# A graph network on one core: an earlier setup for node order and norms, and a last block cut at sixteen tiles

## The chip, the cores and the metric

The kernel runs on one core of a Trainium2 chip. The metric is the device time of one execution in microseconds (us); smaller is better. Three runs of the kernel before gave 6527.34, 6536.39 and 6536.92 us, so the median is 6536.39. The profile is of one further execution, which took 6532.44 us.

A core has five engines that run their own instruction queues side by side: PE (TensorE, matrix products; its weight loads are listed as PEld), DVE (VectorE), ACT (ScalarE), POOL (GpSimd) and SP (SyncE, which here only starts transfers). A transfer (DMA) is started by an engine's queue and then runs on the DMA engines. SBUF is the on-chip memory of 128 partitions; PSUM holds the results of PE.

## The reference: one mean-aggregating layer, then three attention layers over the same graph

There are 6250 nodes with 64 features and 206250 edges sorted by destination. Cut to what matters:

```python
h = relu(layernorm(x))
msg = relu(concat([h[dst], edge_attr_16]) @ W1 + b1)      # layer 0
x = x + relu(segment_mean(msg, dst) + h @ Wres + bres)
h = relu(layernorm(x))
for l in range(3):                                        # 2, 2 and 1 heads
    q, k, v, e = h @ Wq + bq, h @ Wk + bk, h @ Wv + bv, edge_attr_32 @ We
    alpha = sum(q[dst] * (k[src] + e)) / sqrt(C)
    a = segment_softmax(alpha, dst)
    h = segment_sum(a * (v[src] + e), dst) + h @ Ws + bs
    if l < 2: h = prelu(h)
x = x + h
```

## The kernel before

**Order of nodes.** The kernel sorts the nodes by degree into NB = 49 blocks of 128, one node for each partition, so that a block of high degree has many edge tiles and a block of low degree few (`CAP` from 66 to 22). A tile is one edge of each of the 128 nodes of a block.

**Setup** is the first `with tc.manual_schedule(...)` of `gnn_kernel`. There the instructions of POOL, PE, ACT, DVE and SP run on each engine in the order in which the program text issues them. Its steps, with the lines that the prediction uses:

- SP loads `dst` (`prev`), `x` into `xs`, layer 0's weights, and `src` by tiles (`sf`). It then loads `w0blk` (L167), the 24 pieces of the attention weights `wl` (L240, L241), copies `x` into columns 128 to 191 of the DRAM table `tabx` (L242), loads `dst` moved by one (`cur`, L244), `slope` (L245) and 12 pieces of `wblk` (L249).
- PE spreads the first `dst` of each run of 256 edges over all partitions (L185). ACT (L199) and DVE (L194) count from it where seven groups of nodes begin. POOL fetches those stretches of `dst` with seven indirect transfers (L212) into `got`.
- For each of the seven stretches ACT casts it into `looks` (L229) and DVE finds the nodes' first edges in it (L230). ACT sums the squares for the norms of `x`, 49 of them (L225), two behind each stretch and the rest after a last count (L199); then comes the square root (L236).
- DVE turns first edges into degrees and degrees into classes, and counts the classes (L284). PE sums the counts over partitions (`pc`, L286 and L287). DVE scans (L298 to L303) and gets the place of each node in the order (L308 to L321). In between it takes the reciprocal for the norms (L306) and `negr` (L307).
- DVE builds one-hot matrices `to` (L370), `blk` (L372) and `val` (L375, stored over `raw`), in two parts of 24 and 25 columns. PE multiplies them, 49 products that add up in `pperm` (L379). All are 16-bit, and `to` and `val` are read with a step of 49 elements, 98 bytes. DVE reads the sum (`join`, L382) and makes from it, for every block, where each node's edges start (`at_i`, L383) and which node it is (`num_i`, L386).
- The rows of `x` are normalized and projected in 13 groups of four blocks ("quads"): `norm` on ACT (L335) for even quads and on POOL (L332) for odd ones, `turn` (four transposes on PE, L340, and an ACT copy with a relu, L342), `project` (PE L348, ACT copy L350, transfer to `tabx` L351). Rounds 0 to 3 stand in the program ahead of the first part of the 49 products, 4 to 6 ahead of the second, and 7 to 14 behind `join`.
- `sff`, the tiles of `src` as floats (POOL L254), is transposed by PE in 13 pieces (L398), cast by ACT (L401) and written by SP to the flat list `srcs` (L402). This comes last, behind all quads. POOL at last makes `ws` (L406 to L409).

The program tells the end of SP's transfers through eight counters in turn, so a transfer also waits in SP's queue until the one eight places ahead of it has landed: the third `w0blk` transfer waits for `x`.

**Layer 0** (`layer0`) loads edge features, rows of `tabx` and parts of `srcs` by indirect transfers of POOL (all of them at L466, in `pick`): first `load_e(0)`, `load_x(0)`, `load_e(1)` and so on. DVE begins with two memsets (L642), the checks of degrees (L645 and on), 41 small compares (L659) and a comparison of `prev` with `cur` (L666, L667), and then adds up messages.

**Attention** (`attention`) runs three times over the blocks in the order 0, 48, 1, ..., 47. `fetch` gathers one row of keys and values per tile by an indirect transfer of POOL (L466); `scores` takes chunks of up to eight tiles (PE product L809; DVE L817 to L827), `sums` does the softmax and the weighted sum (ACT L849, DVE L841 to L877), and `process` ends a block (L893 to L909). In layers 1 and 2 the block's result is then projected and written to the next layer's table (L914 to L920), and the next layer's gathers wait for that write. In layer 1 a small cast after each chunk (L830) also stores where the sources stand in the new order. The last block, 47, has 24 tiles, the last of them the node itself, which is not gathered. It is done in two parts whose softmaxes are joined:

```python
chunks[end] = [(t, min(CT, cut - t)) for t in range(0, cut, CT)] + [(cut, CAP[end] - cut)]   # cut = 21
parts = [chunks[b][:-1], chunks[b][-1:]] if b == end else [chunks[b]]
```

so the parts are 8 + 8 + 5 tiles and 3 tiles.

Of the kernel before, what the change touches and what calls it, by code (L numbers as in the profile page):

```python
# [22 lines left out]
F32 = mybir.dt.float32  # L23
BF16 = mybir.dt.bfloat16
I32 = mybir.dt.int32
# [54 lines left out]
assert sum(FIN0) == NB  # L80
# [17 lines left out]
def gnn_kernel(ctx: ExitStack, tc: tile.TileContext, x, src_t, dst_t, dst_row, ea16, ea32, eaT16, eaT32, w, out):  # L98
# [17 lines left out]
    with tc.manual_schedule(engines={getattr(mybir.EngineType, e) for e in ("Pool", "PE", "Activation", "DVE", "SP")}), \  # L116
# [6 lines left out]
        val = raw.bitcast(F16)[:, :4 * NB * NB].rearrange("p (v c b) -> p v c b", v=4, b=NB)  # L123
# [16 lines left out]
        sf = p.tile([P, T], I32, name="sf")  # L140
        nc.sync.dma_start(sf, src_t)
# [11 lines left out]
        nc.vector.memset(eps, 1e-5)  # L153
        iota(P, 0, f=col)
# [6 lines left out]
        make_identity(nc, ident)  # L161
# [4 lines left out]
        for j in range(8):  # L166
            nc.sync.dma_start(k.w0blk[j * 16:(j + 1) * 16, j % 4 * D:(j % 4 + 1) * D], w["L0_gnn_W1"][D:, :])  # L167
        nc.gpsimd.memset(ones, 1.0)
# [7 lines left out]
        for t in k.ht:  # L176
            nc.gpsimd.memset(t[D:D + 1, :], 1.0)

# [5 lines left out]
        for c in range(WR):  # L184
            nc.tensor.matmul(pb[:, c, :NW], first[:, c:c + 1].to_broadcast([NW, P]), ident[:NW, :NW],  # L185
                             start=True, stop=True)
        run = p.tile([P, NG0], F32, name="run")
# [30 lines left out]
        negm = p.tile([P, NB], F32, name="negm")  # L218
        var = p.tile([P, NB], F32, name="var")
        nc.vector.tensor_reduce(negm, xs, axis=AX.X, op=OP.add)  # L220
        nc.vector.tensor_scalar(negm, negm, -1.0 / D, None, op0=OP.mult)

        def squares(b):
            sq = p2.tile([P, D], F32, name="sq0")
            nc.scalar.activation(sq, xs[:, b], AF.Square, bias=negm[:, b:b + 1], accum_out=var[:, b:b + 1])  # L225

        place_i = p.tile([P, NG0, 8], U32, name="place_i")
        for g in range(NG0):
            nc.scalar.copy(looks[:, g, :LOOK], got[g])  # L229
            nc.vector.max_index(place_i[:, g], node[:, SG * g:SG * g + 8], looks[:, g])  # L230
            for b in range(2 * g, 2 * g + 2):
                squares(b)
        signs(got[NG0 - 1], NB, less, [P, LOOK], BF16)
        for b in range(2 * NG0, NB):
            squares(b)
        nc.scalar.activation(var, var, AF.Sqrt, bias=eps[:, 0:1], scale=1.0 / D)  # L236

        for l in range(LAYERS):
            for i, s in enumerate("qkvs"):
                nc.sync.dma_start(wl[l][:D, i * D:(i + 1) * D], w[f"L1_gnn_W{s}{l}"])  # L240
                nc.sync.dma_start(wl[l][D:D + 1, i * D:(i + 1) * D], w[f"L1_gnn_b{s}{l}"][None, :])  # L241
# [3 lines left out]
        nc.sync.dma_start(slope, w["L1_gnn_prelu_a"][None, :].to_broadcast([P, 1]))  # L245
        for l in range(LAYERS):
            nc.gpsimd.memset(k.wblk[l], 0.0)
            for j in range(4):
                nc.sync.dma_start(k.wblk[l][j * 32:(j + 1) * 32, j * D:(j + 1) * D], w[f"L1_gnn_We{l}"])  # L249
# [3 lines left out]
        sff = p.tile([P, T], F32, name="sff")  # L253
        nc.gpsimd.tensor_copy(sff, sf)  # L254
        for t, values in ((k.cap, CAP), (least, LEAST)):
            for v, i, j in runs(values):
                nc.gpsimd.memset(t[:, i:j], float(v))
# [26 lines left out]
        nc.vector.tensor_reduce(cnt, oh, axis=AX.X, op=OP.add)  # L284
        pc = pp.tile([P, 2, CLS], F32, name="pc")
# [18 lines left out]

        negr = p.tile([P, NB], F32, name="negr")
        nc.vector.reciprocal(var, var)  # L306
        nc.vector.tensor_mul(negr, negm, var)  # L307
# [15 lines left out]

        hn = p.tile([P, NB, D], F32, name="hn")
        to_tab = tabx.rearrange("(p b) f -> p b f", b=NB)
        quads = [range(b, min(NB, b + 4)) for b in range(0, NB, 4)]
        pts, rxs = {}, {}

        def norm(q):
            for b in quads[q]:  # L330
                if q % 2:
                    nc.gpsimd.tensor_scalar(hn[:, b], xs[:, b], var[:, b:b + 1], negr[:, b:b + 1],  # L332
                                            op0=OP.mult, op1=OP.add)
                else:
                    nc.scalar.activation(hn[:, b], xs[:, b], AF.Identity, bias=negr[:, b:b + 1], scale=var[:, b:b + 1])  # L335

        def turn(q):
            pts[q] = psum.tile([D, 4 * P], F32, name="pr_t")
            for i, b in enumerate(quads[q]):
                nc.tensor.transpose(pts[q][:, i * P:(i + 1) * P], hn[:, b, :], ident)  # L340
            n = len(quads[q]) * P
            nc.scalar.activation(k.ht[q % 2][:D, :n], pts[q][:, :n], AF.Relu)  # L342

        def project(q):
            po = psum.tile([P, 4, 2 * D], F32, name="pr_o")
            n = len(quads[q])
            for i in range(n):
                nc.tensor.matmul(po[:, i, :], k.ht[q % 2][:, i * P:(i + 1) * P], wn, start=True, stop=True)  # L348
            rx = wp.tile([P, 4, 2 * D], F32, name="rx")
# [3 lines left out]
        def rows_of_x(q):  # L353

            if q < len(quads):
                norm(q)
# [1178 lines left out]
```

## Time and profile before

| stage | from, us | to, us | length | DVE busy | POOL busy |
|---|---|---|---|---|---|
| setup (to the first checks of layer 0) | 0 | 121 | 121.0 | 50.7 | 41.5 |
| layer 0 | 121 | 499.5 | 378.5 | 335.6 | 263.8 |
| attention, layer 1 | 499.5 | 2508.9 | 2009.4 | 1034.1 | 1506.1 |
| attention, layer 2 | 2508.9 | 4518.0 | 2009.1 | 1008.8 | 1505.9 |
| attention, layer 3 | 4518.0 | 6530.7 | 2012.7 | 1339.9 | 1511.1 |

The profiled execution has a span of 6530.7 us and took 6532.44 us, so 1.7 us lie around the span. In a line of the timeline or of a group, "out<-in" names what is written from what, "x12" is a count of instructions, and the bracket at the end tells how long the engine stood idle before it and what ended that wait. "SPq" and "POOLq" are the queues that start transfers. An idle time that is put down to "issue" ended with nothing that the profile shows.

### The profile page before, as it was taken

How to read it: one execution, taken by the hardware profiler on the slowest of the kernel's cores; microseconds unless marked ns; L12 is line 12 of the kernel's file. 1: busy time of each engine (PE TensorE's matmuls, PEld its weight loads, DVE VectorE, ACT ScalarE, POOL GpSimd, SP SyncE). 2: the span in 40 equal slices, each digit the busy share in tenths (PEclk: the TensorE clock that was granted, in tenths of full speed). 3: DMA queues.
4: the chain of work that ended last, by engine and by line, in shares of the span. 5: the costliest groups of instructions: out<-in, count | busy, mean ns of one | idle time of the engine just before them, and what ended most of it. 6: DMA issues, size and time to landing. Idle time of an engine off the chain costs nothing. (4 is left out here: it accounts for less than half of the span.)

```text
span 6530.7 us, 28765 instructions
## 1 busy us (share of the span) xinstructions
PE 1956.0 (30%) x5430; PEld 1204.2 (18%) x5430; DVE 3769.0 (58%) x6686; ACT 366.2 (6%) x1266; POOL 4828.3 (74%) x5159
## 2 busy tenths in 40 slices
PE   5762222222222221221222221222333333333342
PEld 3441111111111111111111111111111211121121
DVE  5984545455555553644455545454766666676775
ACT  3220000000000000000000000000000000000000
POOL 4677777777777776777777777776777777777776
PEclk9775555555555555555555555555666666666665
DMA  3674333333333332222222222222222222222222
GB/s 108 221 234 110 81 88 79 85 85 85 83 81 84 83 81 65 72 70 66 69 68 66 69 69 67 70 69 60 71 65 69 65 67 67 67 66 69 65 67 66
DMA packets 242745, 534.93 MB, mean 82 GB/s; under 512 B 101234, under 2 KB 123218, under 8 KB 241458
## 3 DMA queue, kind: packets, MB, share of 16 engines
q0 software_dynamic: 169792, 372.65, 22.7%
q1 hardware_dynamic: 72764, 160.36, 7.8%
q14 instruction: 143, 1.17, 0.1%
q8 instruction: 46, 0.75, 0.0%
HBM read 460.23 MB, written 74.03 MB: 82 GB/s over the span
## 5 line engine op out<-in xcount | busy, mean ns | idle before, releaser
L466 POOL DMA_INDIRECT kv<-tab,src x4788 | 4518.1, 944 | 1499.9 <-issue 1405.9
L820 DVE TENSOR_TENSOR kv<-kv,pe 128x1024 f32<-128x1024 f32 (+7 forms) x666 | 740.1, 1111 | 2237.1 <-DMA kv<-tab,src 2009.4
L809 PE MATMUL pe<-wblk,ea 128*128 128x256 f32 x1740 | 690.6, 553 | 668.4 <-DVE kv L820 598.5
L940 PE MATMUL pos<-only,is_q 128*128 128x448 f32 x616 | 422.6, 799 | 1092.8 <-DVE only L937 1066.8
L914 PE MATMUL pt<-ident,hn 128*64 128x128 f32 x98 | 41.2, 420 | 2131.7 <-DVE hn L909 2110.8
L809 PEld LDWEIGHTS pe<-wblk,ea 128*128 128x128 f32 x1740 | 492.8, 290 | 926.5 <-DVE kv L820 565.3
L866 DVE TENSOR_REDUCE some<-kv 128x64 f32<-128x512 f32 (+3 forms) x693 | 645.4, 931 | 23.9
L809 PE MATMUL pe<-wblk,eaT 128*128 128x256 f32 x870 | 344.7, 561 | 370.7 <-DVE kv L820 347.0
L827 DVE TENSOR_REDUCE al<-prod 128x16 f32<-128x512 f32 (+7 forms) x693 | 438.7, 633 | 24.1
L826 DVE TENSOR_TENSOR prod<-kv,more 128x512 f32<-128x512 f32 (+3 forms) x693 | 438.4, 633 | 24.0
L862 DVE TENSOR_TENSOR kv<-kv,more 128x512 f32<-128x512 f32 (+3 forms) x693 | 431.0, 622 | 0.0
L914 PEld LDWEIGHTS pt<-ident,hn 128*64 128x64 f32 x98 | 12.6, 128 | 2195.4 <-DVE hn L909 2173.8
L940 PEld LDWEIGHTS pos<-only,is_q 128*128 128x128 f32 x616 | 131.6, 252 | 1281.0 <-issue 1087.7
L809 PEld LDWEIGHTS pe<-wblk,eaT 128*128 128x128 f32 x870 | 246.8, 293 | 452.3 <-DVE kv L820 364.7
L947 DVE TENSOR_TENSOR all<-all,pos 128x448 f32<-128x448 f32 x301 | 186.0, 618 | 143.8 <-PE pos L940 135.7
L849 ACT ACTIVATE more<-al,m 128x37 f32<-128x37 f32 (+18 forms) x250 | 73.0, 292 | 2916.1 <-DVE m L844 2891.7
L543 PE MATMUL pm<-w0blk,eT 64*128 64x256 f32 x868 | 171.0, 514 | 91.8 <-DVE msg L546 77.5
L937 DVE TENSOR_TENSOR only<-is_r,more 128x448 f32<-128x448 f32 x308 | 185.1, 613 | 1.5
L466 POOL DMA_INDIRECT e<-in_ea_dram,at_i x98 | 104.9, 1070 | 102.6 <-PE ps L398 39.9
L568 DVE TENSOR_TENSOR msg<-msg 128x128 f32<-128x128 f32 (+12 forms) x221 | 136.2, 616 | 7.1
L543 PEld LDWEIGHTS pm<-w0blk,eT 64*128 64x128 f32 x868 | 110.1, 249 | 136.4 <-DVE msg L546 72.7
L918 PE MATMUL po<-ws,ht 65*128 65x256 f32 x196 | 118.4, 706 | 34.3 <-ACT ht L916 34.3
(217 smaller groups left out, 1737.9 us busy)
## 6 DMA issues: line engine op xcount, KB each, us to landing
kv<-tab,src POOLq DMA_INDIRECT x4788
ea<-eat SPq DMA_DIRECT2D x26, 576.0 KB, 3.8
ea<-eat SPq DMA_DIRECT2D x24, 512.0 KB, 3.4
ea<-eat SPq DMA_DIRECT2D x16, 640.0 KB, 4.0
ean<-e SPq DMA_DIRECT2D x13, 576.0 KB, 3.7
ea<-ean SPq DMA_DIRECT2D x13, 576.0 KB, 4.4
eat<-eaT SPq DMA_DIRECT2D x13, 576.0 KB, 5.6
ea<-eat SPq DMA_DIRECT2D x16, 448.0 KB, 3.4
```

What stands on the lines that cost most here:

```text
L466: return nc.gpsimd.indirect_dma_start(out=out, out_offset=None, in_=table, in_offset=bass.IndirectOffsetOnAxis(ap=idx, axis=0))
L543: nc.tensor.matmul(pm[:, r, u].rearrange("p j f -> p (j f)"), eT[h, t0 // 8 + u, :], k.w0blk[h, :], start=True, stop=True)
L568: nc.vector.tensor_add(msg[:, :h] if c > 2 else total, msg[:, :h], msg[:, c - h:c])
L809: nc.tensor.matmul(pe[:, 4 * (g - g0):4 * (g - g0) + 4].rearrange("p j f -> p (j f)"), ea[:, g, :], k.wblk[l], start=True, stop=True)
L820: nc.vector.tensor_add(pair(kv[:, :m, :2 * D]), pair(kv[:, :m, :2 * D]), pe[:, :m, None, :].to_broadcast([P, m, 2, D]))
L826: nc.vector.tensor_mul(prod[:, :n], kv[:, :n, :D], q[:, None, :].to_broadcast([P, n, D]))
L827: nc.vector.tensor_reduce(als[b][:, :H, t0:t0 + n].rearrange("p h j -> p j h"), prod[:, :n].rearrange("p j (h c) -> p j h c", h=H), axis=A ...
L862: nc.vector.tensor_mul(v.rearrange("p j (h c) -> p j h c", h=H), v.rearrange("p j (h c) -> p j h c", h=H), ex[:, :H, t0:t0 + n].rearrange( ...
L866: nc.vector.tensor_reduce(some[:, i, :], v.rearrange("p j f -> p f j"), axis=AX.X, op=OP.add)
L937: nc.vector.tensor_mul(only, is_r[:, rs, None].to_broadcast([P, SG, D]), res[:, None, :].to_broadcast([P, SG, D]))
L940: nc.tensor.matmul(pos[i].rearrange("p r f -> p (r f)"), is_q, only.rearrange("p r f -> p (r f)"), start=True, stop=True)
L947: nc.vector.tensor_add(all_[:, rs], all_[:, rs], pos.pop(i - 1))
```

## The change

In setup, `make_identity` moves ahead of the first iota on POOL. The loads of `wl`, `slope` and `wblk` (with POOL's memsets of `wblk`) move up in the program to right behind `w0blk`. POOL casts `sff` ahead of the seven indirect transfers; PE transposes it at once into the four PSUM buffers that the quads use later; and ACT casts the four results one by one behind the stretches 0, 1, 3 and 4, each with its transfer by SP, from two buffers `si` in turn. The mean `negm` moves ahead of the counts. For blocks 17 to 48 DVE sums the squares in three large instructions; ACT does blocks 0 to 16 before the first stretch. The square root stands behind stretch 2, the reciprocal and `negr` behind stretch 4. The quads go in a new order `seq`; rounds 0 to 4 stand ahead of the class sums `pc`, and all others ahead of the one-hot matrices, none between or behind the 49 products. `to` and `val` are stored in groups of eight columns, so that PE reads them with a step of 8 elements, 16 bytes; column 48 has tiles of its own, `to1` and `val1`. The memsets of `cap` and `least` move behind the quads in POOL's order, ahead of `ws`.

In attention, the last block's parts are 8 + 8 tiles and 5 + 3 tiles, and its casts for the sources (layer 1) move behind the block's result.

```diff
@@ setup @@
+        make_identity(nc, ident)
         iota(P, 0, f=col)
...
         for j in range(8):
             nc.sync.dma_start(k.w0blk[j * 16:(j + 1) * 16, j % 4 * D:(j % 4 + 1) * D], w["L0_gnn_W1"][D:, :])
+        for l in range(LAYERS):
+            for i, s in enumerate("qkvs"):
+                nc.sync.dma_start(wl[l][:D, i * D:(i + 1) * D], w[f"L1_gnn_W{s}{l}"])
+                nc.sync.dma_start(wl[l][D:D + 1, i * D:(i + 1) * D], w[f"L1_gnn_b{s}{l}"][None, :])
+        nc.sync.dma_start(slope, w["L1_gnn_prelu_a"][None, :].to_broadcast([P, 1]))
+        for l in range(LAYERS):
+            nc.gpsimd.memset(k.wblk[l], 0.0)
+            for j in range(4):
+                nc.sync.dma_start(k.wblk[l][j * 32:(j + 1) * 32, j * D:(j + 1) * D], w[f"L1_gnn_We{l}"])
...
+        nc.gpsimd.tensor_copy(sff, sf)
...
+        nc.vector.tensor_reduce(negm, xs, axis=AX.X, op=OP.add)
+        nc.vector.tensor_scalar(negm, negm, -1.0 / D, None, op0=OP.mult)
...
+        turned = []
+        for t0 in range(0, T, 4 * P):
+            ps = psum.tile([P, 4, P], F32, name="ps", tag=("pr_t", "pr_o")[t0 // (4 * P) % 2])
+            for i, n in enumerate(whole_tiles):
+                nc.tensor.transpose(ps[:n, i, :], sff[:, t0 + i * P:t0 + i * P + n], ident)
+            turned.append((t0, len(whole_tiles), whole_tiles[-1], ps))
+        def flat_src():
+            t0, n, m, ps = turned.pop(0)
+            si = p2.tile([P, 4, P], I32, name="si")
+            nc.scalar.copy(si[:m, :n], ps[:m, :n])
+            nc.sync.dma_start(srcs[...], si[:m, :n])
+        NS = 17
+        nc.vector.tensor_add(hn[:, NS:], xs[:, NS:], negm[:, NS:, None].to_broadcast([P, NB - NS, D]))
+        nc.vector.tensor_mul(hn[:, NS:], hn[:, NS:], hn[:, NS:])
+        nc.vector.tensor_reduce(var[:, NS:], hn[:, NS:], axis=AX.X, op=OP.add)
+        for b in range(NS):
+            squares(b)
         for g in range(NG0):
             nc.scalar.copy(looks[:, g, :LOOK], got[g])
             nc.vector.max_index(place_i[:, g], node[:, SG * g:SG * g + 8], looks[:, g])
-            for b in range(2 * g, 2 * g + 2):
-                squares(b)
+            if g == 2:
+                nc.scalar.activation(var, var, AF.Sqrt, bias=eps[:, 0:1], scale=1.0 / D)
+            elif turned:
+                flat_src()
+            if g == 4:
+                nc.vector.reciprocal(var, var)
+                nc.vector.tensor_mul(negr, negm, var)
         signs(got[NG0 - 1], NB, less, [P, LOOK], BF16)
...
+        seq = [1, 3, 0, 5, 2, 7, 4, 9, 6, 11, 8, 10, 12]
         nc.vector.tensor_reduce(cnt, oh, axis=AX.X, op=OP.add)
+        EARLY = 5
+        for i in range(EARLY):
+            rows_of_x(i)
         nc.tensor.matmul(pc[:, 0, :], ones, cnt, start=True, stop=True)
...
+        for i in range(EARLY, len(seq) + 2):
+            rows_of_x(i)
-        to = p.tile([P, P, NB], F16, name="to")
+        to = p.tile([P, NB // 8, P, 8], F16, name="to")
+        to1 = p.tile([P, P], F16, name="to1")
...
-            for q in ((0, 1, 2, 3), (4, 5, 6))[i]:
-                rows_of_x(q)
...
-        for q in range(7, len(quads) + 2):
-            rows_of_x(q)
@@ attention @@
-        cut = LEAST[end]
-        chunks[end] = [(t, min(CT, cut - t)) for t in range(0, cut, CT)] + [(cut, CAP[end] - cut)]
+        cut = (CAP[end] - 1) // CT * CT
+        chunks[end] = chunks[end][:cut // CT] + [(cut, CAP[end] - 3 - cut), (CAP[end] - 3, 3)]
...
-                    nc.vector.tensor_copy(k.src[1][:, OFF[b] + t0:OFF[b] + t0 + m], kv[:, :m, 2 * D])
+                    places.append((k.src[1][:, OFF[b] + t0:OFF[b] + t0 + m], kv[:, :m, 2 * D]))
+                    if b != end:
+                        nc.vector.tensor_copy(*places.pop())
...
-            parts = [chunks[b][:-1], chunks[b][-1:]] if b == end else [chunks[b]]
+            parts = [chunks[b][:-2], chunks[b][-2:]] if b == end else [chunks[b]]
...
             nc.vector.scalar_tensor_tensor(hn, hn, 0.0, neg, op0=OP.max, op1=OP.add)
+            while places:
+                nc.vector.tensor_copy(*places.pop())
```

## The prediction, made before the changed kernel was run

> **What bounds the kernel now.** I read the engines' totals first, then the waits of setup, then setup's timeline, and last the ends of the three attention layers. The totals:
>
> ```profile
> PE 1956.0 (30%) x5430; PEld 1204.2 (18%) x5430; DVE 3769.0 (58%) x6686; ACT 366.2 (6%) x1266; POOL 4828.3 (74%) x5159
> L466 POOL DMA_INDIRECT kv<-tab,src x4788 | 4518.1, 944 | 1499.9 <-issue 1405.9
> ```
>
> In attention POOL issues one gather every 0.944 + 0.30 us without a break; the change does not touch this. Layer 0 is DVE's (335.6 of 378.5 us busy) and moves as a whole with its start. So the change can act on the 121 us of setup and on the three layer ends. The waits of setup (total, times, longest):
>
> ```profile
> DVE join L382 <- PE pperm L379: 22.8, 1, 22.8
> DVE ht L642 <- PE pr_o L348: 16.5, 1, 16.5
> DVE eps L487 <- DMA srcs<-si: 8.4, 1, 8.4
> POOL e L466 <- PE ps L398: 39.9, 1, 39.9
> POOL rx L466 <- DMA srcs<-si: 5.7, 1, 5.7
> ```
>
> DVE and POOL both wait at the end, first for the 49 products, then for the quads and the turning of `src` behind them. The timeline:
>
> ```profile
> 26.59 10.41 SPq L244 DMA_DIRECT2D rows<-in_dst_row_dram  x2
> ...
> 64.46 10.33 PE L379 MATMUL pperm<-raw,to 128*128 128x196 f16 x24 [4.34 <-DVE raw L375]
> ...
> 82.26 10.78 PE L379 MATMUL pperm<-raw,to 128*128 128x196 f16 x25
> ...
> 93.08 0.36 DVE L382 COPY join<-pperm 128x196 f32<-128x196 f32 x1 [22.77 <-PE pperm L379]
> ...
> 114.40 1.02 POOL L466 DMA_INDIRECT e<-in_ea_dram,at_i  x1 [39.90 <-PE ps L398]
> ...
> 120.53 0.21 DVE L645 TENSOR_TENSOR no<-deg,cap 128x49 f32<-128x49 f32 x1
> ```
>
> PE works almost without a gap from 64.5 to 112; from `join` to layer 0's first check 27.4 us pass, of which DVE needs about 2.5. The ends of layers 1, 2 and 3 (DVE's first instruction on the five-tile chunk; the bracket is the idle time ahead of it):
>
> ```profile
> 2491.00 0.82 DVE L820 TENSOR_TENSOR kv<-kv,pe 128x640 f32<-128x640 f32 x1 [0.16 <-DMA kv<-tab,src]
> ```
> ```profile
> 4500.14 0.82 DVE L820 TENSOR_TENSOR kv<-kv,pe 128x640 f32<-128x640 f32 x1 [2.92 <-DMA kv<-tab,src]
> ```
> ```profile
> 6509.36 0.82 DVE L820 TENSOR_TENSOR kv<-kv,pe 128x640 f32<-128x640 f32 x1 [3.63 <-DMA kv<-tab,src]
> ...
> 6521.98 0.98 POOL L472 DMA_INDIRECT out_dram<-hn,num_i  x1 [6.56 <-POOLq L413]
> ```
>
> In layers 2 and 3 DVE idles before that chunk lands, and then works 13.5 and 12.3 us in a row to the block's result.
>
> **The change, part by part: up to `negr`.** `make_identity` delays `col` by the 0.4 us that its two instructions take; DVE's cast behind it has until 7.83, when the first `dst` lands. POOL's memsets of `wblk` (0.82) and cast of `sff` (1.52, from `sf`, landed before 13.6) fit into its idle time from 8.5 to 19.8; if `sf` came after 18 the seven fetches would wait. The 13 transposes (3.1) lie on an idle PE. `negm` (3.42 + 0.39) starts when `x` lands, 11.4 by the third `w0blk` transfer, and ends at 15.2; the counts began at 14.78 behind ACT. So +0.4 for everything behind. ACT's 17 squares (0.333 each) run from 15.2 to 20.9 beside the fetches. DVE's three large ones cost 6.9 (1617 elements took 1.84 us, so 2048 take 2.3), to about 27; its searches (1.0 each) fall behind by 2 us and catch up by stretch 3.
>
> Then the queue that was moved past. SP must issue 24 `wl`, `slope` and 12 `wblk` (0.44 each) before the first `srcs`: `wl` ends at 26.0 as now, `wblk` at 32 to 33.5. ACT's third cast of `src` needs the first `si` free, so that transfer landed: 2.4 us later (in the profile the third cast waits from the issue at 112.34 to 114.81), at 34.5 to 36. Behind it in ACT's queue stand stretches 4, 5 and 6 and the last count, which DVE waits for. With 0.7 a stretch and 0.5 a cast, `negr` is ready at 37.7 to 38.9; I take 38.3. DVE's degree chain starts near 40 instead of 37.82, +2.3. The fetches themselves get faster, because `tabx<-x` and `cur` (landing 12.6, SP held for 10 us) come after them; but ACT is held longer than they were. A root amid counts may ask for another table load: 0 or 1.28 us; I take 0, since layer 0 shows squares and roots in turn without one.
>
> **Class sums.** PE now does four `turn` and three `project` before `pc`. POOL's first quad takes 4 x 0.63 (14 took 9.06 beside DVE; alone 0.39, over all 24 0.83), so PE starts at 40.8; 4 x 1.06 + 3 x 1.91 + 1.0 = 11 us later, at 52, `pc` is done. DVE's scan ends at 47.8 + 0.25 + 2.1 = 50.2, so a new wait of 2 us. Against it 1.65 us go (L306, L307 and their wait for the root). DVE's part of the matrices thus ends about 2.5 us later than now, 70.3 + 2.5 + 0.6 for the three new instructions on column 48 = 73.4. If groups of eight cost these 16-bit instructions their rate, it were twice the 8.2 us of L370 and L375 per part at most, 81; they read unit steps before and after, so I take no loss.
>
> **Quads and products.** Nine more quads at PE's pace of 2.56 (74.60, 77.14, 79.70 in the profile) and a short one end at 52 + 24 = 76. ACT needs 3.6 us for two quads, PE 5.1; SP's `rx` transfers queue behind `cur` until 48, three buffers cover that. So PE, not DVE, sets the start of the 49 products: 76. They take 0.4255 each now. With a step of 16 bytes instead of 98 the trace shows nothing. Upper end: no change, 20.9 us in all. Lower end: PE loads 128 weights of the same tile at the same step in 0.148 us, 1.16 ns each, so 196 columns in 0.227, 11.1 us. The nearest row is the product itself, and f32 products at unit step do not run faster per column (128 columns at 0.239, 1.87 ns against 2.17); I take no change. `join` comes at 76 + 20.9 + 0.1 = 97.0, 3.9 later than now.
>
> [...]
>
> **Behind `join`.** Nothing is left there. DVE's six small instructions take 1.36, two memsets 1.02: layer 0's first check at 99.4 instead of 120.53, -21.1. POOL's `cap`, `least` (1.66) and `ws` (2.1) lie in its wait for `join`. `e` for block 0, issued near 98.4 and landing 5.2 later, is there before DVE ends its 11 us of checks, so DVE's time decides.
>
> **Layer ends.** The first part's softmax (4.3 us) now fits ahead of the five-tile chunk. DVE works on without the idle time, but has one more small sum (0.25). Layer 2: 2.92 - 0.25 = 2.7; layer 3: 3.63 - 0.25 = 3.4; the last gathers land 1.7 us after issue and are not late. Layer 1 has no idle time there (0.16): three casts leave (0.35), one sum comes (0.25), 0.1. Ends: between no gain (if the chunk is late by what was saved) and 6.6; I take 6.2.
>
> **Sum.** 21.1 + 6.2 = 27.3 off the profiled execution's own 6532.4 gives 6505. That execution lies 4.0 under the median of the three runs.
>
> **Rivals.** (A) PE reads faster at the shorter step: the products take 0.227, 9.8 us less, 6495. For it: the weight row above; against it: the f32 rows. [...] (B) The gain in setup is mostly eaten before `join`: a second hold such as SP's 10.41 (L244) ahead of `srcs` and POOL at 0.83 in the chain, +11.5, 6517. Against it: the long transfers stand behind `srcs` now. (C) The ends give nothing, the split being late by its own second part: 6511. (D) Slower: the gathers. Nothing in the change speeds them, but 4788 of them stand in a row; should the new layout make each 9 ns longer than 1.244 us, that is 43 us and 6548. It decides from 27.3/4788 = 5.7 ns. Against it: three layers with different tables took 2009.4, 2009.1 and 2012.7, within 0.2%.
>
> **How the numbers follow.** Forecast 0.45, A 0.36, B 0.09, C 0.05, D 0.05. The runs before differ by 0.15%, so about 0.2%, 13 us, is what a measurement can tell. Forecast, A and C lie beyond it on the fast side, B on either side of it (half each with 6519 to 6527 in reach), D beyond it on the slow side or within: faster 0.88, same 0.07, slower 0.05. The range reaches from A less 10 (the fastest run before lies 5 under the profiled one; quads 5 faster), 6485, to B, 6518.
>
> **What would show it.** Right: ACT's third `si` waits on a `srcs` transfer near 30 to 36; `pc` near 52; L379 in one run from about 76; `join` near 97 with no PE work behind it but layer 0's; DVE at L645 near 99; 2.9 and 3.6 us of idle gone at the ends. Wrong: L379 at well under 0.42 a product (A), `join` past 105 (B), `kv` gathers over 950 ns (D).

## The result, and the profile after

The changed kernel takes 6502.74 us (median of five runs, 6500.48 to 6506.85), the kernel before 6536.39 (five runs, 6527.34 to 6542.28): a ratio of 0.9949, 95% interval 0.9937 to 0.9962. The forecast was 6505 in a range of 6485 to 6518. The total was right; several steps under it were not, and they cancel. The profiled execution took 6500.48 us with a span of 6498.5, against 6532.44 and 6530.7.

The totals and the gather row of the changed kernel's page:

```profile
PE 1949.3 (30%) x5430; PEld 1200.3 (18%) x5430; DVE 3774.5 (58%) x6695; ACT 354.3 (5%) x1202; POOL 4838.8 (74%) x5159
L499 POOL DMA_INDIRECT kv<-tab,src x4788 | 4527.6, 946 | 1498.8 <-issue 1321.8
```

The gathers took 9.5 us more than before (4518.1): 946 ns each instead of 944. By stage the two profiled executions compare as follows, in us, each number the distance between two starts in the trace. "Again" is a second execution of the changed kernel, from the experiments.

| stage | before | after | again | forecast of the change |
|---|---|---|---|---|
| start to layer 0's first check | 120.53 | 86.23 | 91.32 | -21.1 |
| layer 0, to the first kv gather | 379.04 | 375.68 | 375.89 | 0 |
| the gathers of three layers, first to last | 5973.6 | 5983.5 | 5973.2 | 0 |
| last gather to the next layer's first, or to the end, three ends | 57.6 | 53.0 | 50.8 | -6.2 |
| span | 6530.7 | 6498.5 | 6491.2 | -27.3 |

Setup gained 34.3, not 21.1. The gathers took 9.9 back. Setup of the changed kernel in its timeline:

```profile
19.95 2.28 DVE L262 TENSOR_TENSOR hn<-x,negm 128x2048 f32<-128x2048 f32 x1
20.12 3.12 POOL L236 DMA_INDIRECT rows<-in_dst_row_dram,run_i  x1 [4.94 <-DVE run_i L231]
22.27 2.29 DVE L263 TENSOR_TENSOR hn<-hn 128x2048 f32<-128x2048 f32 x1
23.55 1.83 POOL L236 DMA_INDIRECT rows<-in_dst_row_dram,run_i  x1 [0.30 <-issue]
25.69 0.95 POOL L236 DMA_INDIRECT rows<-in_dst_row_dram,run_i  x1 [0.30 <-issue]
...
31.53 1.28 ACT L272 ACT_TABLE_LOAD   x1
...
36.26 0.59 ACT L254 CAST si<-ps 128x512 int32<-128x512 f32 x1 [2.41 <-DMA srcs<-si]
...
39.04 0.21 DVE L277 TENSOR_TENSOR negr<-negm,var 128x49 f32<-128x49 f32 x1
...
41.08 0.29 DVE L333 TENSOR_TENSOR start<-place_i,run 128x49 f32<-128x49 uint32 x1
...
67.61 17.21 PE L423 MATMUL pperm<-raw,to 128*128 128x196 f16 x49
...
84.85 0.36 DVE L426 COPY join<-pperm 128x196 f32<-128x196 f32 x1 [10.74 <-PE pperm L423]
...
86.23 0.21 DVE L678 TENSOR_TENSOR no<-deg,cap 128x49 f32<-128x49 f32 x1
```

The forecast's hold is there (ACT's third cast waits 2.41 us for the first `srcs`). So are two things that it did not have: the first two fetches take 3.12 and 1.83 us beside DVE's large instructions, and the root's table load (1.28 us) now stands among the stretches. Both lie ahead of the hold. The load in the kernel before:

```profile
49.86 1.28 ACT L236 ACT_TABLE_LOAD   x1
```

The 49 products start at 67.6, not 76, and are 0.351 us apart, not 0.426.

PE's stretches in setup, two of 2 us each while the quads run and three during the products (the columns: stretch, its length, PE's busy time and matrix instructions, granted clock, DMA share, GB/s):

```profile
50.00:52.00 2.00, 2.00 (x12) 1.00 0.38 113
56.00:58.00 2.00, 2.00 (x20) 1.00 0.46 131
68.00:70.00 2.00, 2.00 (x7) 1.00 0.80 233
72.00:74.00 2.00, 2.00 (x7) 0.50 0.00 0
80.00:82.00 2.00, 2.00 (x7) 0.50 0.00 0
```

Two readings. First, the quads went from 12 to 20 instructions per stretch. The trace's first clock record of this execution opens at 53.78 us (full) and the next at 70.84 (half): TensorE's clock stepped up in the middle of the quads. Ahead of the first record the column reads 1.00 too, with 12 instructions where there are 20 behind it, so the 1.00 at 50 us is no measurement. The eight projections of a quad take 1.91 us ahead of the step and 1.06 to 1.16 behind it, and 1.91 to 1.92 all through the setup of the kernel before, whose first record lies at 129.36 us: I read that as a low clock there too. Second, the products did not care: 7 per stretch at 1.00 and at 0.50.

The layer ends (DVE's first instruction on the five-tile chunk in layers 1, 2 and 3, and the last scatter):

```profile
2461.11 0.82 DVE L853 TENSOR_TENSOR kv<-kv,pe 128x640 f32<-128x640 f32 x1
```
```profile
4471.68 0.82 DVE L853 TENSOR_TENSOR kv<-kv,pe 128x640 f32<-128x640 f32 x1
```
```profile
6481.24 0.82 DVE L853 TENSOR_TENSOR kv<-kv,pe 128x640 f32<-128x640 f32 x1
...
6489.67 0.98 POOL L505 DMA_INDIRECT out_dram<-hn,num_i  x1 [3.12 <-POOLq L446]
```

The idle time ahead of the chunk is gone in all three (these lines have no bracket). From the last gather to the block's result DVE took 13.8, 13.7 and 12.4 us before and 13.8, 11.5 and 9.0 after: layer 1 gained nothing.

### The profile page after: what moved, and what is told of

Read it like the earlier page. It is cut to its first block, busy times and chain, and to the rows that moved or that the text cites. A ratio compares the mean times of both kernels' runs of the same rounds, so it can differ in the third digit from the quotient of the medians.

```text
span 6498.5 us, 28713 instructions
## 1 busy us (share of the span) xinstructions
PE 1949.3 (30%) x5430; PEld 1200.3 (18%) x5430; DVE 3774.5 (58%) x6695; ACT 354.3 (5%) x1202; POOL 4838.8 (74%) x5159
## 5 line engine op out<-in xcount | busy, mean ns | idle before, releaser
L499 POOL DMA_INDIRECT kv<-tab,src x4788 | 4527.6, 946 | 1498.8 <-issue 1321.8
L951 PE MATMUL pt<-ident,hn 128*64 128x128 f32 x98 | 41.1, 420 | 2137.8 <-DVE hn L944 2117.0
L955 PE MATMUL po<-ws,ht 65*128 65x256 f32 x196 | 119.5, 713 | 34.3 <-ACT ht L953 34.3
```

Source lines behind the costliest of these rows:

```text
L499: return nc.gpsimd.indirect_dma_start(out=out, out_offset=None, in_=table, in_offset=bass.IndirectOffsetOnAxis(ap=idx, axis=0))
```

## The experiments

Questions: does the pace of the gathers and of the quads belong to the program or to the execution; what made the products faster; what do the layer ends give; what was missed ahead of the degree chain; can what was missed be had.

**The changed kernel again, unchanged.**

> The changed kernel once more, unchanged. In the profile of the changed kernel each of the 4788 kv gathers took 946 ns and the three rows of 1596 gathers were 1994.5 us long; before the change it was 944 ns and 1991.2 us, 9.9 us in all. Theory G (an execution has its own pace, the program has none): this second execution gives another pace, anywhere between 944 and 947 ns, so 4518 to 4532 us for the row. Rival H (the changed program makes every gather 2 ns longer): 946 ns and 1994.5 us a layer again, within 0.3 us. For the TensorE: before 53.8 us the quads were paced at 2.56 us and behind it at 1.8. If that step belongs to the work on TensorE, it comes again at 50 to 57 us; if it is chance, it comes elsewhere or not at all, and then the quads end near 76 instead of 67.8 and `join` comes at 93.

Its gather row and two stretches of the quads:

```profile
L499 POOL DMA_INDIRECT kv<-tab,src x4788 | 4517.8, 944 | 1495.8 <-issue 1407.6
```
```profile
50.00:52.00 2.00, 2.00 (x12) 1.00 0.65 188
56.00:58.00 2.00, 2.00 (x12) 1.00 0.44 131
```

944 ns, 1991.1 us a layer: the pace of the gathers belongs to the execution. No step of the clock in the quads either (12 instructions in both stretches, 1.91 us for eight projections), the products from 72.67 (the quads were expected to end near 76) and `join` at 89.94 (93 expected). The span is 6491.2, 7.3 below the first profile of the same program: 10.3 less in the gathers and 2.2 in the ends, 5.1 more in setup, where the clock stayed low. This execution took 6493.18 us and the kernel before, run beside it, 6525.11: 31.9 less, one run each.

**The new layout alone, on the kernel before; and the old layout in the changed kernel.**

```diff
-        to = p.tile([P, P, NB], F16, name="to")
+        to = p.tile([P, NB // 8, P, 8], F16, name="to")
+        to1 = p.tile([P, P], F16, name="to1")
```

(`val` likewise, and the reverse in the other kernel.)

> The kernel before with `to` and `val` in groups of eight and nothing else. Theory S (the step in memory sets the pace of the 49 products: 0.426 us at 98 bytes, 0.351 at 16): products 0.35 us apart, each of the two parts 1.8 us shorter, `join` at 93.1 - 3.7 = 89.4 and layer 0's first check at 116.8. Theory T (the pace was better only because TensorE's clock had been opened by the quads ahead): 0.426 us again, `join` at 93. Rival on DVE: if groups of eight cost the 16-bit instructions on DVE their rate, those of the first part take more than the 5.8 us they took.

> The changed kernel with the old layout of `to` and `val` (step 98 bytes) and all else as changed. Theory S (step): products 0.426 us apart, the row of 49 takes 20.9 instead of 17.2 us, `join` at 88.5, layer 0's first check at 89.9. Theory T (clock): 0.351 us as in the changed kernel, `join` at 84.9.

The products of the first kernel, then those of the second:

```profile
65.29 8.62 PE L394 MATMUL pperm<-raw,to 128*128 128x196 f16 x24 [4.56 <-DVE raw L384]
81.38 8.79 PE L394 MATMUL pperm<-raw,to 128*128 128x196 f16 x25
90.21 0.36 DVE L397 COPY join<-pperm 128x196 f32<-128x196 f32 x1 [18.44 <-PE pperm L394]
```
```profile
73.23 20.94 PE L408 MATMUL pperm<-raw,to 128*128 128x196 f16 x49
94.21 0.36 DVE L411 COPY join<-pperm 128x196 f32<-128x196 f32 x1 [16.30 <-PE pperm L408]
95.59 0.21 DVE L663 TENSOR_TENSOR no<-deg,cap 128x49 f32<-128x49 f32 x1
```

0.352 us with a step of 16 bytes, 0.426 with 98, in both directions, with the clock low in both kernels (1.91 us for eight projections in each). The step sets it; the clock does not, by the 7 products per stretch at 1.00 and at 0.50 above. `join` missed what was expected for other reasons: 90.21 for 89.4 in the first kernel, whose degree chain began 0.6 us later than in the first profile, and 94.21 for 88.5 in the second, where the clock did not step up and the products began at 73.2. The weight load is not what fell: its mean is 0.145 us at 16 bytes and 0.148 at 98. How much of the rest of a product is the reading of its 196 columns the traces do not tell, since they show weights being loaded while a product runs (in the second kernel a load from 81.71 to 81.85 within a product from 81.70 to 82.31). DVE paid nothing clear: the row of `val` for the first part took 3.06 us (3.00 before). In the totals the layout alone is not seen: 6525.10 us against 6525.11 for the kernel before, one run each.

One product more tells whether the step of 16 bytes is free. The last, for column 48, reads `to1` and `val1`, which have no step at all. In the changed kernel, at half clock, 24 products with a step of 16 bytes and then this last one (mean ns behind the comma):

```profile
L423 PE MATMUL pperm<-raw,to 128*128 128x196 f16 x24 | 8.6, 531 | 0.0
L423 PE MATMUL pperm<-raw,to 128*128 128x196 f16 x1 | 0.3, 347 | 0.0
```

These times overlap and their ends are modelled, but the starts say the same: in the first kernel of this pair PE's next instruction starts 0.140 us after the last product, at 89.96, where the products before it start 0.352 apart; in the kernel before, whose last product has a step of 98 bytes too, it starts 0.426 after. So the step of 16 bytes is a good part of what a product costs. With all 49 at unit step they would take about 7 to 8 us instead of 17.2; this is an estimate from 0.140 and from 0.351 less the 0.184 between the two rows, and what DVE would pay to write them so no run shows.

**The last block's parts alone, on the kernel before.**

```diff
-            parts = [chunks[b][:-1], chunks[b][-1:]] if b == end else [chunks[b]]
+            parts = [chunks[b][:-2], chunks[b][-2:]] if b == end else [chunks[b]]
```

(with the chunks and the late casts that go with it)

> The kernel before with the new parts of the last block alone. By the traces of the pair: from the last kv gather of a layer to the first of the next (or to the end) 18.4, 16.5 and 18.1 us instead of 18.1, 18.0 and 21.4, so 4.5 us less in all. By the prediction's count 6.2 less. If the gain at the ends came from something in setup, nothing. The gathers: 944 ns if the pace belongs to the program of before, anything from 944 to 947 if each execution has its own.

From the last gather to the result: 10.5, 11.6 and 9.1 us; the three ends together 49.6, so 8.0 less than the 57.6 of the kernel before (4.5 expected from the pair, 6.2 by the prediction). Here layer 1 gained 3.3, which it did not in the changed kernel. The two differ in when SP issues the next layer's first `ea` transfers (1088 and 384 KB). DVE's start on the second eight-tile chunk and that issue, first in the changed kernel, then in this one:

```profile
2447.69 0.98 SPq L809 DMA_DIRECT2D ea<-eat  x2
2453.73 1.22 DVE L853 TENSOR_TENSOR kv<-kv,pe 128x1024 f32<-128x1024 f32 x1 [8.57 <-DMA kv<-tab,src]
```
```profile
2478.61 0.98 SPq L776 DMA_DIRECT2D ea<-eat  x2
2480.39 1.22 DVE L820 TENSOR_TENSOR kv<-kv,pe 128x1024 f32<-128x1024 f32 x1 [5.28 <-DMA kv<-tab,src]
```

Counted from the last gather (2456.39 and 2486.32) the transfers were issued 8.7 us ahead in the first and 7.7 in the second, and DVE could start on the chunk 2.7 us ahead in the first and 5.9 in the second. The same pair in other executions: issued 8.57 ahead, start 2.68 (before, layer 1); 8.28 and 2.86 (again, layer 1); 7.42 and 5.87 (again, layer 2). In the transfer view of the changed kernel, gathers issued up to 2445 land in 2.5 us, and the one issued behind the `ea` transfers takes 5.7. The `ea` transfers had been issued 1.2 and 0.5 us ahead of it. This made a theory for the next experiment.

**The `ea` transfers held back, on the changed kernel.**

```diff
+            if l and b in order[:2]:
+                nc.scalar.copy(flat[:, :1], k.rows[:, end, :1])
             nc.sync.dma_start(flat, (k.ean if l == 0 else k.eat)[:, g])
```

> The changed kernel with the first two ea transfers of layers 2 and 3 (1088 and 384 KB) held until the last block's row is copied, instead of being issued as soon as the buffers come free, 7.4 to 8.7 us ahead of the last gather. Theory C (they hold up the last gather of the second chunk of eight, so that DVE starts on that chunk 2.7 us ahead of the last gather instead of 6, and the first part's softmax no longer fits ahead of the chunk of five): the result of layer 1 comes 10.5 us after the last gather instead of 13.6 to 13.8, that of layer 2 10.5 instead of 10.5 to 11.5, layer 3 as before at 9.0 to 9.1; the next layer's gathers then start 14.6 us after the last instead of 17.7 to 18.4 and 14.9 to 16.5. Rival D: the next layer's first block waits for its ea, DVE falls behind and the row of 1596 gathers is longer than 1991.2 by what was won.

```profile
2454.57 1.22 DVE L855 TENSOR_TENSOR kv<-kv,pe 128x1024 f32<-128x1024 f32 x1 [5.48 <-DMA kv<-tab,src]
2461.94 0.82 DVE L855 TENSOR_TENSOR kv<-kv,pe 128x640 f32<-128x640 f32 x1
...
2474.29 0.79 SPq L811 DMA_DIRECT2D ea<-eat  x2
2475.95 0.94 POOL L499 DMA_INDIRECT kv<-tab,src  x1 [14.72 <-issue]
```

The chunk starts 5.7 and 5.8 us ahead of the last gather in layers 1 and 2, the results come 10.8 and 10.6 us after it as expected, and the next layers start after 15.7 and 15.3 us (14.6 expected; from result to start it takes 4.7 to 4.9 here, 4.1 to 4.4 in the second execution). The row of 1596 gathers stays at 1991.0 to 1991.2, so rival D did not come. The collision is shown; it was in the kernel before as well, hidden there behind the wait for the five-tile chunk.

**Four buffers for the turned `src`.**

```diff
-            si = p2.tile([P, 4, P], I32, name="si")
+            si = p2.tile([P, 4, P], I32, name="si", bufs=4)
```

> The changed kernel with four buffers for the turned src instead of two. Theory (the prediction's step: ACT's third cast waits for the first srcs transfer, 2.4 us, and the stretches behind it are held): no such wait, DVE's degree chain starts 2.4 us earlier, at 38.3 instead of 40.7 to 41.1, the quads too, `join` at 87.5 and layer 0's first check at 88.9 instead of 91.3 (compared with the execution in which TensorE's clock stayed low in setup). Rival: the last fetch lands no earlier than the hold ends, and the chain starts where it did, within 0.5 us.

```profile
38.25 0.29 DVE L333 TENSOR_TENSOR start<-place_i,run 128x49 f32<-128x49 uint32 x1
...
88.89 0.21 DVE L678 TENSOR_TENSOR no<-deg,cap 128x49 f32<-128x49 f32 x1
```

As expected to 0.1 us, and `join` at 87.52. The hold on ACT cost 2.4 us against the second execution, passed on whole to the end of setup. The six executions with the hold on ordinary chips start the chain at 40.7 to 41.5, so 2.4 is the lower end.

**DVE's large instructions behind the first search.**

```diff
-        nc.vector.tensor_add(hn[:, NS:], xs[:, NS:], negm[:, NS:, None].to_broadcast([P, NB - NS, D]))
 (and the square and the sum)
+            if g == 0:
+                nc.vector.tensor_add(...)   (the same three)
```

> The changed kernel with DVE's three large instructions on x (difference, square, sum of 2048 elements) behind the first search instead of ahead of it. In both executions of the changed kernel the first two fetches took POOL 3.12 and 1.82 us, the other five 0.95; before the change 1.14 and six times 0.95. Theory P (POOL is slowed while DVE runs the difference and the square, 2.28 us each): all seven at 0.95 to 1.15, the last issued at 27.5 to 28 instead of 30.4. Rival Q (the first fetches are slow for another reason, such as transfers in flight): 3.1 and 1.8 again. The sum then ends on DVE near 33, so the root on ACT waits, and degree chain and `join` come within 1 us of where they were.

```profile
25.90 2.27 DVE L269 TENSOR_TENSOR hn<-x,negm 128x2048 f32<-128x2048 f32 x1
26.50 2.49 POOL L236 DMA_INDIRECT rows<-in_dst_row_dram,run_i  x1 [0.30 <-issue]
28.20 2.29 DVE L270 TENSOR_TENSOR hn<-hn 128x2048 f32<-128x2048 f32 x1
29.30 2.02 POOL L236 DMA_INDIRECT rows<-in_dst_row_dram,run_i  x1 [0.30 <-issue]
```

The slowness moved with the instructions: the first five fetches take 1.15 and 0.95, the sixth and seventh 2.49 and 2.02. The mechanism of theory P holds; its size here does not (I had expected all seven to be out of the way by then, and the last one is over at 31.3 us as it was). The degree chain started at 40.07 and the first check came at 90.7, both 0.6 earlier than in the second execution, less than the 0.8 by which executions differ. A fetch that starts beside the difference or the square ends 0.8 to 1.0 us after that instruction, in all four places; the sum (L264 in the changed kernel, 2.29 us) slows none: the fetch that starts beside it there takes 0.95.

**`src` turned late again.**

```diff
-        turned = []   (13 transposes ahead of the searches, casts among them)
+        turned = []   (the same behind `join`)
```

> The changed kernel with src turned behind the products again, as before the change; the norms, the quads and the layout stay early. Theory (src turned early is worth what stood behind join for it: 13 transposes 3.1, casts, four transfers and their landing, 10 us in the kernel before from the first transpose to layer 0's first check): layer 0's first check 6 to 9 us later than in the unchanged execution, 97 to 100, less the 2.4 us that ACT is no longer held by the srcs transfers. Rival (layer 0 needs srcs late, it is hidden): within 1 us of 91.3 or earlier by 2.4.

```profile
80.49 0.36 DVE L408 COPY join<-pperm 128x196 f32<-128x196 f32 x1 [9.64 <-PE pperm L405]
...
89.47 0.06 DVE L520 MEMSET eps<- 128x1 f32 x1 [7.62 <-DMA srcs<-si]
89.54 0.21 DVE L678 TENSOR_TENSOR no<-deg,cap 128x49 f32<-128x49 f32 x1
```

The first check came at 89.5, not at 97 to 100, but this does not speak for the rival. In this execution the clock stepped up at 44.8 us (21 matrix instructions in the 4 us from 40, 30 in the 4 us from 46), so the quads ended at 62 and the products followed DVE's matrices. Behind `join` 9.05 us pass instead of 1.38, of which DVE waits 7.62 for `srcs`: that is what `src` turned late costs. The chain ahead starts at 37.96 instead of 40.68, as in the kernel with four buffers. With a low clock, by these numbers, the products would have started 2.7 us ahead of the 72.67 of the second execution, and the first check would be at 91.3 - 2.7 + 7.7 = 96.3; this is worked out, not measured.

**The kernel before again.**

> The kernel before once more, unchanged, to see which of its stages repeat. Profiled first: layer 0's first check at 120.5, layer 0 until the first kv gather 379.0 us, each layer's 1596 gathers 1991.2, the three ends 57.6 in all. In the four executions since, layer 0 took 373.5 to 375.9 us. If layer 0's length belongs to the execution (TensorE's clock steps at other moments each time), it comes out at 373 to 379 here; if it belongs to the start time in the program of before, at 379 again. Setup: 119.5 to 121. TensorE's clock: no step in setup (it came at 129 us).

This execution, and the three kernels just shown, ran on a third chip, where everything up to layer 0 is as elsewhere (first check at 119.9) but attention is not: 7780.24 us in all. POOL's gathers take 951 ns there, but POOL also stands idle for 991 us until DVE is done with a buffer (the row by lines, with the shares of its idle time):

```profile
L466 POOL DMA_INDIRECT kv<-tab,src x4788 | 4555.0, 951 | 2613.4 <-issue 1510.0 <-DVE some L866 991.2 <-DMA tab<-rows 70.2
```

What holds DVE up on that chip stays open. The change shows there all the same: 7780.46 for the kernel before, 7735.0 to 7741.57 for the three variants of the changed kernel, one run each. Layer 0's length can't be compared there (428 us). On the ordinary chips it was 379.0, 374.5 and 375.2 us in the profiles of the kernels without the early quads and 372.3 to 377.3 in seven with them, so the 3.4 us that layer 0 seems to have gained are the spread of executions.

**More work on TensorE ahead of the quads.** Six executions of kernels with early quads had shown the step of the clock twice. The quads issue without a gap, but the trace gives the shape of their transposes as 128*64 and of their projections as 65*128, where the added products have 128*128.

```diff
+            if g < 5:
+                for i in range(12):
+                    nc.tensor.matmul(pperm.rearrange("p v b -> p (v b)")[:, :P], ident, looks[:, g, :P], start=True, stop=True)
```

> The changed kernel with 60 more f32 products on TensorE (128 x 128 x 128, twelve behind each of ACT's first five casts of stretches, into a PSUM tile that the first of the 49 products clears). In six executions of kernels with the early quads TensorE's clock stepped up during the quads twice (at 53.8 and 44.8 us) and four times not. [...] Theory A (the step needs more of the array in use than the quads give; they are just at the edge): with full-size products it steps up between 27 and 41 us, the quads come 1.8 us apart instead of 2.56 and end at 60 to 63 instead of 72.5, the products then wait for DVE's matrices, `join` at 83.5 to 84.5 and layer 0's first check at 85 to 86 instead of 91.3. Rival (chance, whatever TensorE does): no step, the quads end at 72 to 73, the first check at 91 or up to 1 us later for the added products.

Stretches of PE, the first two during the added products, the third during the quads:

```profile
28.00:31.00 3.00, 3.00 (x16) 0.50 0.92 316
32.00:35.00 3.00, 3.00 (x30) 1.00 1.00 299
46.00:50.00 4.00, 3.82 (x34) 1.00 0.94 246
```

The step comes between 31 and 32 us (0.50 with 16 instructions in the 3 us from 28, 1.00 with 30 in the 3 us from 32), 4.4 to 5.4 us after the first added product (26.62) and within the 27 to 41 of theory A, and the pace stays up to the end of the quads (1.16 us for eight projections at 63.20). They end at 65.9, later than the 60 to 63 expected since the added products ran until 42.5; the products then wait only for DVE's matrices, `join` comes at 83.6 and the first check at 84.97. In all, eight executions on the changed kernel and its variants with quads alone showed the step twice (44.8 and 53.8), with the same instructions ahead of it. One execution with added full-size products showed it where it was called for, and in the next one, below, the quads have the fast pace from their start. These two fit theory A, against two of eight without; no run varied the share of the array at the same amount of work, so that the share decides, and that the quads lie just at the edge, is argued and not shown.

**Everything together, and the changed kernel beside it.** On top of the changed kernel: four buffers, 42 added products, the `ea` transfers held back, and 30 instead of 17 squares on ACT (so that DVE's large instructions are 1216 elements long).

```diff
-        NS = 17
+        NS = 30
```

> Everything that the runs pointed to, in one kernel on top of the changed one: four buffers for the turned src, 30 instead of 17 squares on ACT (so DVE's large instructions beside the fetches are 1216 elements long), 42 full-size products on TensorE behind the first four casts, and the two ea transfers at the layer ends held until the last row is copied. Theory (each acts where it was seen to act): TensorE's clock steps up by 35, DVE's degree chain starts at 37 to 38.3, the products wait only for DVE's matrices, `join` at 79.5 to 82, layer 0's first check at 81 to 83.5 instead of 91.3; the three layer ends 49 instead of 50.8 to 53. Against the changed kernel 10 to 13 us less, 0.15 to 0.2%; against the kernel before a ratio of 0.992 to 0.994. Rival: the end of setup is then set by something else (the x rows on SP, the lists), and the first check stays above 85; or layer 0, whose length varied from 373.5 to 379 us, gives it back.

> The changed kernel unchanged, timed in rounds on the same chip as the kernel with everything added, for the comparison of the two. 0.9945 to 0.9955 of the kernel before; whether TensorE's clock steps up in setup is open (one of two executions of it did), with `join` at 85 if it does and at 90 if not.

6487.44 us (five runs, 6481.74 to 6495.79), a ratio to the kernel before of 0.9936 (0.9923 to 0.995); the changed kernel beside it 6495.94 (6492.32 to 6498.36), 0.9951 (0.9937 to 0.9964), with `join` at 90.7, near the 90 expected without a step of the clock. 8.5 us less by the medians, with intervals that overlap: it beats the kernel before, and beats the changed kernel only by the look of it. The profile says where the rest went:

```profile
36.48 0.28 DVE L337 TENSOR_TENSOR start<-place_i,run 128x49 f32<-128x49 uint32 x1
...
49.36 0.59 ACT L317 COPY rx<-pr_o 128x512 f32<-128x512 f32 x1 [3.57 <-DMA tabx<-rx]
...
50.34 1.41 PE L307 MATMUL pr_t<-ident,hn 128*64 128x128 f32 x4 [2.96 <-ACT hn L302]
```

The degree chain starts at 36.5, 4 to 5 us earlier than in the changed kernel, and the clock is up when the quads start (1.16 us for eight projections at 39.43, as with the added products alone). But the quads now come so early that the fourth `rx` needs its buffer while the first, issued at 43.5, is still on its way. It lands 5.9 us after its issue (2.3 in the kernel before, issued at 58.2); that it stands behind the 1568 and 768 KB of `tabx<-x` and `cur`, issued from 36.8 on, is read from the order of the issues. ACT waits 3.57 us, PE stands idle for 2.96, and behind that the quads have the pace of the low clock (2.08 and 1.92 us for eight projections at 51.81 and 54.53, 1.06 at 46.31). They end at 69.0, the first check comes at 87.5 instead of the expected 81 to 83.5. The rival that named the x rows on SP was right. The layer ends gave what they should, 49.3 us in all. The profiled execution was the slowest of its five (6495.79) and had the slower gathers, 4528.7 us in all against 4517.8 in the second execution of the changed kernel.

## Why the prediction was right, and where it was not

**Up to `negr`: right in the mechanism, short by 0.5 to 1.0, and lucky in what it left out.** The hold of ACT's third cast is there and it sets the time. From its end to `negr` the sum had about 3.0 us, and 2.99 passed. What was short is the end of the hold: the first `srcs` was issued at 32.5 and landed at 36.3 (33.1 and 35.9 in the second execution), where the sum had 34.5 to 36. So `negr` was ready at 39.2 (38.8) for 38.3, and the degree chain started at 41.1 (40.7) for 40. Two wrong statements cost nothing here because the hold covered them. "The fetches themselves get faster" was wrong: the first two got slower, by 2.9 us, because DVE's large instructions were moved beside them; I had costed DVE's time and never asked who else they stop. And the root did take a table load of 1.28 us, put at 0 in the sum though the kernel before has one ahead of its root too; no further one came. Ahead of the third cast ACT still idled 2.41 us (1.70). Where the hold is gone, they stand in the way: with four buffers ACT waits 1.07 us for the third fetch and then goes through the load to the next stretch without a gap, and the chain starts at 38.25; with everything together, where the first two fetches took 2.26 and 0.96 us, it starts at 36.48.

**Class sums: the new wait of 2 us is not there.** `pc` was done at 50.5, not 52: PE started at 39.9 on the first block of POOL's first quad, where the sum had it wait to 40.8 for all four. DVE's scan ended at 51.6, after it, for 50.2. DVE's matrices were ready at 73.44, forecast 73.4: by luck the lateness of the chain made up for the wait that did not come. The groups of eight cost nothing, as taken; the upper bound named for them, "the 8.2 us of L370 and L375 per part", does not come out of the profile, where they are 5.0 and 5.2 us a part and 10.2 in both.

**Quads: 76 was too late.** With a low clock the products behind them start at 72.7 (second execution). Of the 3.3 us, 2.0 are the earlier `pc`, done at 50.0 there, and the rest is a count of 24 us for what took 22.6. With the step of the clock they ended at 67.8. That the clock could step up at all the prediction did not have; the kernel before showed none of it in setup.

**Products: the term that was mis-sized.** Taken at 0.426, it is 0.351, with both ends of the bracket (0.426 and 0.227) known; "well under 0.42" was the sign named for rival A. A's mechanism was right and its size was not; the nearest row that I chose by, f32 at unit step, was no guide to f16 at 98 bytes. A step of 8 elements is not free: 0.351 at either clock, and 531 ns beside the 347 of the one product at unit step.

**Behind `join`: right,** 1.38 for 2.4, since the two memsets of 0.48 found room earlier. With the quads and the products that puts the first check at 86.2, or 91 to 92 in the executions without a step, where I had 99.4. So of the 13.2 us by which setup beat the forecast, about 5 are the step of the clock (91.3 - 86.2), 3.7 the products, 3.3 the end of the quads and 1 the memsets.

**Layer ends: layer 3 right (3.3 to 3.4), layer 2 0.7 to 3.1 for 2.7 in three executions of the changed kernel, layer 1 nothing, as said, but for another reason.** I read 0.16 us of idle time as a limit; the chunk of eight ahead of it had been held up by 3 us by the `ea` transfers, and where these came later layer 1 gained 3.3 as well.

**Gathers: rival D's place, not its cause.** The 9.9 us that came back in the profiled pair are 2 ns on each of 4788 gathers, and the second execution of the same program did not have them. With the sum of the executions that had the ordinary pace and no step (setup 91.3 to 92.1 against 119.9 to 120.5, three ends 51 to 54 against 58) the change is worth 31 to 36 us, of which 27.3 were forecast. The measured 6502.74 lies between the forecast (6505, 0.45) and A (6495, 0.36), and that it lies so near the forecast is in part luck. In the profiled execution the span fell by 32.2 us for 27.3: 13.2 more than forecast in setup and 3.4 in layer 0, which is its spread, against 9.9 lost in the gathers and 1.6 at the ends. Of the other four runs there is no trace.

## What to carry to other kernels

When a large instruction is moved, ask not only what waits for its engine but what it stops beside it: here DVE's difference and square of 2048 elements (2.28 and 2.29 us) held two of POOL's fetches up, which took 3.12 and 1.83 us instead of 0.95. Then ask whether the path feels it: here another wait covered it. Where columns are read with a step, look for a row at unit step before calling a shorter step free (here 347 ns against 531 at 16 bytes). Read an idle time of nothing at one place as a question about the instruction ahead of it: a transfer issued a microsecond earlier by an engine off the path had moved the wait there. And before reading 10 us out of a pair of profiles of 6500, take a second execution: the changed kernel ran its gathers at a mean of 946 ns in one and at 944 in the other.

## What the runs showed of the hardware

- f16 products on PE with 196 columns came 0.426 us apart at a step of 98 bytes and 0.351 at 16, the latter the same at full and half granted clock; their weight loads took 0.148 and 0.145. The one at unit step took 347 ns where those with 16 bytes took 531 and those with 98 took 612.
- During the quads TensorE's clock stepped up at 53.8 us in the first execution of the changed kernel, 14 us after they began, and not at all in the second (12 instructions in 2 us from 50 and from 56). With full-size f32 products ahead of the quads it stepped up, in one execution, 4.4 to 5.4 us after the first of them.
- The granted clock reads 1.00 ahead of the trace's first record (53.78 us) with 12 matrix instructions in 2 us, and 1.00 behind it with 20.
- A POOL indirect transfer that otherwise takes 0.95 us took 1.82 to 3.12 when it started beside DVE's difference or square of 2048 elements in f32, and ended 0.8 to 1.0 us after it.
- A gather that lands in 2.5 us took 5.7 behind two transfers of 1088 and 384 KB issued 1.2 and 0.5 us earlier.
- The 4788 kv gathers took POOL 4518.1 and 4517.8 us in the kernel before and in the second execution of the changed one (944 ns each), and 4527.6 and 4528.7 in its first execution and with everything together (946): 10 to 11 us a run, where the runs of the kernel before differ by 15.
